# A context attention that keeps 32 keys: wider weights and masks, three small operations moved, the last group turned in two parts

## The chip, the cores and the metric

The kernel runs on one core of one Trainium2 chip, as one launch. Its time is the device time of that core in microseconds (us). TensorE multiplies matrices into PSUM, VectorE does elementwise work and reductions, ScalarE functions and copies, GpSimd (POOL in the profile) elementwise work on SBUF; SyncE (SP) issues most DMAs. In the profile PEld is TensorE's loading of the stationary operand, DVE is VectorE and ACT is ScalarE.

## What is computed

The reference is a small network of two layers on 4 batches of 256 tokens, with 4096 context tokens of 192 numbers a batch. The change lies in one step, the context attention of the second layer. Cut to that step:

```python
Q = (x_text @ Wq).reshape(Bb, Tt, H, DH)            # H = 4 heads of 32
K = (x_vision @ Wk).reshape(Bb, Gg, H, DH)          # 4096 keys from 192 numbers each
scores = jnp.einsum('bthd,bghd->bhtg', Q, K) / np.sqrt(DH)
scores = jnp.where(vision_mask[:, None, None, :], scores, -jnp.inf)
topv, topi = jax.lax.top_k(scores, 32)
probs = jax.nn.softmax(topv, axis=-1)
attn = jnp.zeros_like(scores).at[bi, hi, ti, topi].set(probs)
attn_mean = attn.mean(axis=1)                       # over the heads
V = x_vision @ Wv
c_t = jnp.einsum('btg,bgd->btd', attn_mean, V) * text_mask[..., None]
```

Each token and head keeps the 32 best of 4096 keys, and the softmax runs over these alone. `c_t` then steers the rest of the layer. Everything is in float32 except the mask.

## The kernel before

The step is `l1_context`, with `l1_context_keys` for the keys. It runs over 32 **units**: 4 batches, 2 tiles of 128 tokens, 4 heads. The four heads of one tile form a **group**; there are 8 groups. A unit goes through these steps:

- `scores(u)` (TensorE, two halves `c2` of 2048 keys): the 4096 scores of 128 tokens. Each half fills two PSUM tiles of 128x1024; ScalarE copies each to SBUF (`sc`, L1164). The pool `x1_sc` has eight such tiles, so two units' worth. The PSUM pool `big` has two tiles, so a half can begin only as the tiles of the half before are copied.
- `best(u, part)` (VectorE): the 8 largest of every 128 scores, 16 operations of 128 elements for each half (L1176).
- `chosen(u)`: from these 256 candidates VectorE takes the 32 best, 8 at a time (L1184, L1189). After the first 8 it writes `neg`, minus the largest score (L1187). ScalarE then takes the exponential of all scores with `neg` as bias, in four operations of 1024 (L1191), and of the 32 best (`e32`, L1193).
- `weighted(u)` (VectorE): the mask, in four operations of 1024 (L1200): a weight stays where its score is at least the 32nd best. Then the sum of `e32` (L1202), its reciprocal (L1203), and the factor 0.25 for the mean over the heads times the token's `keep` flag (L1204). POOL writes `diag`, the identity scaled by that number for each token (L1206).
- `gathered` (once a group, in four steps `c4` of 1024 keys): TensorE turns the weights of all four heads with `diag` as the moving operand (L1219), which transposes, scales and sums over the heads at once. ScalarE copies the result (`wT`, L1227) and TensorE multiplies it with the context (`cx`, L1233) into one PSUM tile `ps_c`. It yields after each turning and after each product, so a group is eight pieces. At its end come a copy `o`, a check `off` on VectorE (L1241) and a DMA of `o` to `c.cn`.

The weights of one group fill all sixteen tiles `e`. `weights(u)` hands the tiles out row by row in one group and column by column in the next, so that a unit of the next group may write its exponentials as soon as one step `c4` of the running `gathered` has read its tiles.

The order of the work is written out by hand in the loop over `u`: `chosen(u)`, first half of `best(u + 1)`, `weighted(u)`, second half of `best(u + 1)`, one piece of the running `gathered` (`late`), first half of `scores(u + 2)`, one piece of `late`, second half of `scores(u + 2)`, then one or two pieces of `keys(b + 1)` for the next batch. At the fourth head of a group what is left of `late` is run out and the group just weighted becomes the new `late`. After the last unit nothing is left beside the last group's `gathered` but loads for the next stage, which begins with a branch on `c.bad` and reads `c.cn`. The framework beneath places the semaphores by the parts of tiles that operations touch, and may move operations of one engine past each other when it plans the order.

`keys(b)` makes the keys of one batch in eight chunks of 512: the 192 context numbers are contracted as 128 rows (L1049) and as 64 rows (L1050), the latter from the upper or the lower half of the array by turns. The context comes by `context_keys` in tiles of 128 x 1536 numbers, four a batch, two buffered (L247); `load_kk` loads the weights for this layout with three DMAs. ScalarE copies each chunk (`ks`, L1052) and SP writes it to the `kt` tile in four DMAs (L1054). The first batch's keys are made before `l0_ffn`, the others beside the units.

Of the kernel before, what the change touches and what calls it, by code (L numbers as in the profile page):

```python
# [11 lines left out]
F32 = mybir.dt.float32  # L12
# [9 lines left out]
P = 128  # L22
# [209 lines left out]
def mask_rows(c, pool, mu):  # L232
# [10 lines left out]
def context_keys(c, pool, b, c4, queue=None):  # L243


    t = pool.tile([P, 1536], F32, tag="ctxT", name="ctxT")
    (queue or c.nc.sync).dma_start(t, c.a["ctxT"][b, c4])  # L247
    return t


def load_kk(c, pool, name, queue=None):
# [770 lines left out]
def l1_context_keys(c, es):  # L1022

    nc, tc = c.nc, c.tc
    w = Ctx()
    one = es.enter_context(tc.tile_pool(name="x1_kt", bufs=1))
    two = es.enter_context(tc.tile_pool(name="x1_ks", bufs=2))
    w.psum = es.enter_context(tc.tile_pool(name="x1_ps", bufs=1, space=PSUM))
    w.wk = load_kk(c, one, "x1_wku")
    w.wq = load_k(c, one, "x1_wq4")  # L1030
    w.keep = load(c, one, "x1_keep", [P, NB], dt=U8)
    w.kts = [one.tile([P, 4, G // 4], F32, tag=f"kt{i}", name=f"kt{i}") for i in range(2)]

    w.mask = one.tile([P, G // 4], BF16, tag="mask", name="mask")
    nc.vector.memset(w.mask, 0.0)
    w.pick = one.tile([P, B, P], BF16, tag="pick", name="pick")
    for b in range(B):
        nc.sync.dma_start(w.mask[b:P:32, :], c.mrowb[b].rearrange("(j k) -> j k", j=4))
        nc.vector.tensor_copy(w.pick[:, b, :], c.cols[:, 5 + b : 6 + b].to_broadcast([P, P]))

    def keys(b):

        kt = w.kts[b % 2]
        for c4 in range(4):
            ctxT = context_keys(c, two, b, c4)
# [12 lines left out]

    w.keys = keys
    return w  # L1060


def l1_context(c, w, beside):
# [13 lines left out]
    with ExitStack() as es:  # L1077
# [11 lines left out]
        nc.vector.tensor_copy(keep, w.keep)  # L1089
        off = one.tile([P, NB], F32, tag="off", name="off")  # L1090
# [51 lines left out]
        def scores(u):  # L1142

            b, tt, h = units[u]
            kt = w.kts[b % 2]
            sc[u] = []
            for c2 in range(2):
                cs = slice(c2 * 512, (c2 + 1) * 512)
                pss = [big.tile([P, 2, 512], F32, tag="big", name="ps_s") for _ in range(2)]
                for j in range(4):  # L1150
                    rs = slice(32 * j, 32 * j + 32)
                    nc.tensor.matmul(pss[j // 2][:, j % 2, :], w.pick[rs, b, :], w.mask[rs, cs], start=True, stop=False)
                for j in range(4):
                    rs = slice(32 * j, 32 * j + 32)
                    nc.tensor.matmul(  # L1155
                        pss[j // 2][:, j % 2, :],
                        qs[b][rs, h, tt * P : (tt + 1) * P],
                        kt[rs, h, cs],
                        start=False,
                        stop=True,  # L1160
                    )
                for ps in pss:
                    t = scs.tile([P, 2, 512], F32, tag="sc", name="sc")
                    nc.scalar.copy(t, ps)  # L1164
                    sc[u].append(t)
                yield

        sc, cands = {}, {}
# [1 line left out]
        def best(u, part):  # L1170

            if part == 0:
                cands[u] = two.tile([P, 32, 8], F32, tag="cand", name="cand")
            for n in range(16 * part, 16 * part + 16):
                c4, i = divmod(n, 8)
                nc.vector.max(cands[u][:, n, :], sc[u][c4][:, i // 4, (i % 4) * P : (i % 4 + 1) * P])  # L1176

        def chosen(u):

            top = two.tile([P, 32], F32, tag="top", name="top")  # L1180
            flat = cands.pop(u).rearrange("p n k -> p (n k)")
            for r in range(4):
                t8 = top[:, 8 * r : 8 * r + 8]
                nc.vector.max(t8, flat)  # L1184
                if r == 0:
                    neg = two.tile([P, 1], F32, tag="neg", name="neg")
                    nc.vector.tensor_scalar(neg, top[:, 0:1], -1.0, None, ALU.mult)  # L1187
                if r < 3:
                    nc.vector.match_replace(flat, t8, flat, TAKEN)  # L1189
            for t, src in zip(weights(u), sc[u]):  # L1190
                nc.scalar.activation(t, src, AF.Exp, bias=neg)  # L1191
            e32 = two.tile([P, 32], F32, tag="e32", name="e32")
            nc.scalar.activation(e32, top, AF.Exp, bias=neg)  # L1193
            return top, e32

        def weighted(u, top, e32):

            b, tt, h = units[u]
            for t, src in zip(weights(u), sc.pop(u)):
                nc.vector.scalar_tensor_tensor(t, src, top[:, 31:32], t, ALU.is_ge, ALU.mult)  # L1200
# [5 lines left out]
            nc.gpsimd.tensor_scalar(diag, c.ident, r, None, ALU.mult)  # L1206
            return weights(u), diag

        def gathered(b, tt, es):

            ps_c = acc.tile([P, 512], F32, tag="acc", name="ps_c")
            n = 0
            for c4 in range(4):
                wTs = []
                for half in range(2):
                    ps = pst.tile([P, 512], F32, tag="pt", name="ps_w")
                    for i in range(4):
                        for h, (e, diag) in enumerate(es):
                            nc.tensor.matmul(  # L1219
                                ps[:, i * P : (i + 1) * P],  # L1220
                                e[c4][:, half, i * P : (i + 1) * P],
                                diag,
                                start=(h == 0),
                                stop=(h == 3),
                            )
                    wT = two.tile([P, 512], F32, tag="wT", name="wT")
                    nc.scalar.copy(wT, ps)  # L1227
# [2 lines left out]
                for half, wT in enumerate(wTs):  # L1230
                    for i in range(4):
                        t, j = c4 % 2 * 2 + half, c4 // 2 * 4 + i
                        nc.tensor.matmul(  # L1233
                            ps_c[:, : DC + 1], wT[:, i * P : (i + 1) * P], cxs[b][t][:, j, :], start=(n == 0), stop=(n == 31)
                        )
# [17 lines left out]
        for u, (b, tt, h) in enumerate(units):  # L1253
# [774 lines left out]
def _arrays(i):  # L2028
# [11 lines left out]
    for m in range(P):  # L2040
# [13 lines left out]
    ctxT = i["ctx_768"].transpose(0, 2, 1).reshape(B, DC, 4, 2, 512)  # L2054
    ctxT = np.concatenate(
        [ctxT[:, 0:P].transpose(0, 2, 1, 3, 4).reshape(B, 4, P, 1024), ctxT[:, P:].transpose(0, 2, 3, 1, 4).reshape(B, 4, P, 512)], 3
    )
    return {
        "x": i["x"],
        "ctx": i["ctx_768"],  # L2060
        "ctxT": ctxT,
        "ctx6": i["ctx_768"].reshape(B, 4, 4, 256, 6, 32).transpose(0, 1, 2, 5, 4, 3).reshape(B, 4, P, 6, 256),
        "gmask": i["mask_BxS2_bf1"].view(np.uint8),
        "cols": cols,
# [78 lines left out]
```

## Time and profile before

| what | value |
|---|---|
| median of 3 runs | 2594.22 us (2590.08 to 2595.49) |
| profiled execution | 2598.63 us, of which span 2596.8 us |
| busy over the span | PE 2377.7 us (92%), PEld 1460.1 (56%), DVE 1659.8 (64%), ACT 1064.9 (41%), POOL 145.2 (6%) |
| mean granted TensorE clock | 0.935 |
| first and last mask (L1200) | 1626.3 and 2145.6 us from the start |
| last product with cx (L1233) | ends at 2182.8 us |
| first and last keys chunk | 1507.5 and 1999.9 us |

The page has a strip of the busy tenths of each engine in 40 slices of 65 us. The units lie in slices 26 to 33; the last of these holds the end of the last group:

```
PE   6999999999999999999688989989999988984897
DVE  6666666666666666678544423988888892725644
PEclk7999999999999999999799799999799998996876
```

A matmul of float32 stands as two records in the trace, so L1219 counts 2048 for 1024 matmuls. A row of a group gives the line, engine and operation, what it writes and reads with sizes, the count, then busy time and the mean of one in ns, and last the idle time of the engine ahead of it and what ended that. A row of the order of time gives start, length, the operation, and in brackets the idle time before it. A clock of 0.5 means that TensorE ran at half its speed.

### The profile page before, as it was taken

The page shows a single profiled execution, that of the slowest core. Times are in us where ns is not written, and L with a number is a line of the kernel's source. Part 1 is how long each engine was busy: PE and PEld are TensorE (multiplying, and loading weights), DVE is VectorE, ACT ScalarE, POOL GpSimd, SP SyncE. Part 2 cuts the span into 40 slices and gives each one's busy share as a digit, 9 for nine tenths or more (in the row PEclk, how much of TensorE's full clock was granted, in tenths as well). Part 3 has the DMA queues.
Part 4 walks back from the last instruction along what each step waited for, and adds up shares of the span by engine and source line. Part 5 has one row for each costly group of instructions (what it writes and reads, how often), then busy time and mean ns, then how long its engine had stood idle before and what let it go on. Part 6 is the DMA issues. An engine that isn't in the chain of part 4 may idle for free. (4 is left out here: it accounts for less than half of the span.)

```text
span 2596.8 us, 54625 instructions
## 1 busy us (share of the span) xinstructions
PE 2377.7 (92%) x22673; PEld 1460.1 (56%) x22673; DVE 1659.8 (64%) x4019; ACT 1064.9 (41%) x1865; POOL 145.2 (6%) x176
## 2 busy tenths in 40 slices
PE   6999999999999999999688989989999988984897
PEld 4655555555555555545455535467676777453554
DVE  6666666666666666678544423988888892725644
ACT  1355554555555554556122121755555651010221
POOL 3000000000000000000000000001011010412000
PEclk7999999999999999999799999799999998996876
DMA  8321213121221213000100031202212004000110
GB/s 208 91 57 58 66 49 79 43 75 48 67 56 59 75 40 81 28 8 2 38 5 1 1 116 57 61 27 73 64 51 59 27 27 143 14 1 16 33 25 9
DMA packets 63375, 132.29 MB, mean 51 GB/s; under 512 B 11744, under 2 KB 38560, under 8 KB 62672
## 3 DMA queue, kind: packets, MB, share of 16 engines
q1 hardware_dynamic: 61616, 124.65, 17.1%
q8 instruction: 181, 2.97, 0.5%
q10 hardware_dynamic: 992, 3.02, 0.4%
q0 software_dynamic: 512, 1.05, 0.2%
q14 instruction: 74, 0.61, 0.1%
HBM read 98.17 MB, written 5.34 MB: 40 GB/s over the span
## 5 line engine op out<-in xcount | busy, mean ns | idle before, releaser
L512 DVE TENSOR_REDUCE mx<-ps_a 128x1 f32<-128x512 f32 x1024 | 659.7, 685 | 223.6 <-PE ps_a L497 220.0
L508 ACT ACTIVATE e<-ps_s 128x512 f32<-128x512 f32 x1024 | 555.7, 595 | 418.1 <-PE ps_a L497 397.8
L497 PE MATMUL ps_a<-kt,qa 32*128 32x512 f32 x2048 | 659.5, 647 | 12.0 <-DVE mx L512 8.1
L483 PE MATMUL ps_s<-qb,kt 32*128 32x256 f32 x4096 | 592.4, 401 | 0.0
L483 PEld LDWEIGHTS ps_s<-qb,kt 32*128 32x128 f32 x4096 | 349.6, 184 | 197.5 <-issue 106.6
L425 PE MATMUL o_ps<-e,v 128*32 128x256 f32 x4096 | 327.6, 391 | 0.0
L497 PEld LDWEIGHTS ps_a<-kt,qa 32*128 32x128 f32 x2048 | 230.9, 185 | 41.8 <-DVE mx L512 19.7
L1219 PEld LDWEIGHTS ps_w<-diag,e 128*128 128x128 f32 x2048 | 240.0, 198 | 24.6 <-issue 22.4
L1219 PE MATMUL ps_w<-diag,e 128*128 128x128 f32 x2048 | 245.8, 282 | 1.4 <-POOL diag L1206 1.4
L1176 DVE MAX8 cand<-sc 128x8 f32<-128x128 f32 x1024 | 212.3, 277 | 11.7 <-ACT sc L1164 10.2
L425 PEld LDWEIGHTS o_ps<-e,v 128*32 128x32 f32 x4096 | 81.0, 108 | 246.5 <-issue 235.0
L1200 DVE SCALAR_TENSOR_TENSOR e<-sc,top,e 128x1024 f32<-128x1024 f32 x128 | 159.3, 1279 | 31.9 <-ACT e L1191 31.9
L1191 ACT ACTIVATE e<-sc,neg 128x1024 f32<-128x1024 f32 x128 | 143.1, 1146 | 33.0 <-PE ps_w L1219 32.4
L1164 ACT COPY sc<-ps_s 128x1024 f32<-128x1024 f32 x128 | 126.1, 1006 | 46.2 <-PE ps_s L1155 45.6
L329 PE MATMUL ps_k<-ctxT,x_wk 32*128 32x256 f32 x1536 | 103.3, 398 | 12.3 <-DMA ctxT<-in_ctx 12.3
L351 PEld LDWEIGHTS ps_v<-x_wv,ctxT 32*128 32x128 f32 x3072 | 97.9, 191 | 15.4 <-DVE mx L512 9.4
L351 PE MATMUL ps_v<-x_wv,ctxT 32*128 32x128 f32 x3072 | 105.1, 280 | 0.7
L1233 PEld LDWEIGHTS ps_c<-cx,wT 128*128 128x128 f32 x512 | 88.0, 199 | 27.6 <-ACT wT L1227 11.4
L329 PEld LDWEIGHTS ps_k<-ctxT,x_wk 32*128 32x128 f32 x1536 | 87.7, 194 | 26.8 <-issue 18.2
L1233 PE MATMUL ps_c<-cx,wT 128*128 128x193 f32 x512 | 99.7, 347 | 2.0 <-ACT wT L1227 2.0
L814 POOL TENSOR_TENSOR x<-x,f_bo 128x256 f32<-128x256 f32 x8 | 5.8, 724 | 1547.6 <-DVE x L813 1520.4
L1155 PE MATMUL ps_s<-kt,q 32*128 32x512 f32 x512 | 85.8, 657 | 0.0
(401 smaller groups left out, 2520.0 us busy)
## 6 DMA issues: line engine op xcount, KB each, us to landing
ctxT<-in_ctx SPq DMA_DIRECT2D x62, 768.0 KB
kt<-ks SPq DMA_DIRECT2D x352, 64.0 KB
ctxT<-in_ctxT SPq DMA_DIRECT2D x16, 768.0 KB
cx<-in_ctx SPq DMA_DIRECT2D x16, 768.0 KB
x_w<-in_x_w SPq DMA_DIRECT2D x2, 1024.0 KB
qk<-rot SPq DMA_DIRECT2D x8, 256.0 KB
a_qk<-qk SPq DMA_DIRECT2D x16, 128.0 KB
ctxT<-in_ctx ACTq DMA_DIRECT2D x2, 768.0 KB
```

Source lines behind the costliest of these rows:

```text
L329: nc.tensor.matmul(ps[:, :256], w.wk[hs, gp, k, :], ctxT[hs, k, :], start=(k == 0), stop=(k == 5))
L351: nc.tensor.matmul(ps[:, ks], ctxT[hs, k, ks], w.wv[hs, gp, k, :], start=(k == 0), stop=(k == 5))
L425: nc.tensor.matmul(o_pss[u][32 * h : 32 * h + 32, :S], vs[g // 2][:, c0 : c0 + 32], ew[h][:, n % 2, :], start=(n == 0), stop=(n == GT - 1),)
L483: nc.tensor.matmul(ps[:, k * S : (k + 1) * S], kts[u % 4 // 2][hs, u % 2, ks], qbs[u][hs, :], start=True, stop=True,)
L497: nc.tensor.matmul(ps, qas[u][hs, tt * P : (tt + 1) * P], kts[u % 4 // 2][hs, u % 2, ch * 512 : (ch + 1) * 512], start=True, stop=True,)
L508: nc.scalar.activation(e, ps.rearrange("p (k n) -> p k n", k=2), AF.Exp)
L512: nc.vector.tensor_reduce(mxs[u][:, tt, h, ch : ch + 1], ps, AX.X, ALU.max)
L1176: nc.vector.max(cands[u][:, n, :], sc[u][c4][:, i // 4, (i % 4) * P : (i % 4 + 1) * P])
L1191: nc.scalar.activation(t, src, AF.Exp, bias=neg)
L1200: nc.vector.scalar_tensor_tensor(t, src, top[:, 31:32], t, ALU.is_ge, ALU.mult)
L1219: nc.tensor.matmul(ps[:, i * P : (i + 1) * P], e[c4][:, half, i * P : (i + 1) * P], diag, start=(h == 0), stop=(h == 3),)
L1233: nc.tensor.matmul(ps_c[:, : DC + 1], wT[:, i * P : (i + 1) * P], cxs[b][t][:, j, :], start=(n == 0), stop=(n == 31))
```

## The change

It has five parts, all in the context attention of the second layer.

1. The sixteen tiles `e` become one tile of 16 x 1024, and `sc` becomes four tiles of 2048. Exponentials and masks are done 2048 at a time: two of each a unit in place of four. The score copies stay at 1024 each, two into one tile. `weights(u)` hands out the same places as before.
2. The negation `neg` goes from VectorE to POOL.
3. The sum of `e32` is taken by ScalarE's accumulating output as it computes the exponential; the factor 0.25 and `keep` are multiplied once for all tiles (`quarter`) and enter `diag` on POOL as a second multiplication. VectorE's reduction and its scaling of `r` go.
4. The keys are contracted as twice 96 rows. The context is laid out for that (`ctx96`), loaded in chunks of 96 x 1024 numbers, eight a batch, still two buffered; the weights come in one DMA.
5. The last group (units 28 to 31) is turned in two parts. At units 29 and 30 two more pieces of `late` are run each, at unit 30 the group before is run out, and the first two heads are turned and multiplied with `cx` while the last heads are still being chosen. The last two heads follow, and add to the same PSUM tile.

```diff
-    w.wk = load_kk(c, one, "x1_wku")
+    w.wk = one.tile([96, 2, P], F32, tag="x1_wku", name="x1_wku")
+    nc.sync.dma_start(w.wk, c.a["x1_wku"].rearrange("(k p) n -> p k n", p=96))
...
-            ctxT = context_keys(c, two, b, c4)
             for j in range(2):
-                hs = slice(64 * j, 64 * j + 64)
+                ctx = two.tile([96, 2, 512], F32, tag="ctx", name="ctx")
+                nc.sync.dma_start(ctx, c.a["ctx96"][b, 2 * c4 + j])
                 ps = w.psum.tile([P, 512], F32, tag="mm", name="ps_k")
-                nc.tensor.matmul(ps, w.wk[:, 0, :], ctxT[:, j * 512 : (j + 1) * 512], start=True, stop=False)
-                nc.tensor.matmul(ps, w.wk[hs, 1, :], ctxT[hs, 1024:1536], start=False, stop=True)
+                for k in range(2):
+                    nc.tensor.matmul(ps, w.wk[:, k, :], ctx[:, k, :], start=(k == 0), stop=(k == 1))
...
-        scs = last.enter_context(tc.tile_pool(name="x1_sc", bufs=8))
+        scs = last.enter_context(tc.tile_pool(name="x1_sc", bufs=4))
...
+        nc.vector.tensor_scalar(quarter, keep, 0.25, None, ALU.mult)
...
-        tiles = [ews.tile([P, 2, 512], F32, tag=f"e{i}", name=f"e{i}") for i in range(16)]
+        tiles = ews.tile([P, 16, 1024], F32, tag="e", name="e")
...
-            return [tiles[4 * c4 + h if odd else 4 * h + c4] for c4 in range(4)]
+            return tiles[:, h:16:4, :] if odd else tiles[:, 4 * h : 4 * h + 4, :]
...
-                for ps in pss:
-                    t = scs.tile([P, 2, 512], F32, tag="sc", name="sc")
-                    nc.scalar.copy(t, ps)
-                    sc[u].append(t)
+                t = scs.tile([P, 2, 1024], F32, tag="sc", name="sc")
+                for j, ps in enumerate(pss):
+                    nc.scalar.copy(t[:, j, :], ps.rearrange("p q n -> p (q n)"))
+                sc[u].append(t)
...
-                    nc.vector.tensor_scalar(neg, top[:, 0:1], -1.0, None, ALU.mult)
+                    nc.gpsimd.tensor_scalar(neg, top[:, 0:1], -1.0, None, ALU.mult)
...
-            for t, src in zip(weights(u), sc[u]):
-                nc.scalar.activation(t, src, AF.Exp, bias=neg)
+            for part, src in enumerate(sc[u]):
+                nc.scalar.activation(weights(u)[:, 2 * part : 2 * part + 2, :], src, AF.Exp, bias=neg)
...
-            nc.scalar.activation(e32, top, AF.Exp, bias=neg)
+            nc.scalar.activation(e32, top, AF.Exp, bias=neg, accum_out=r)
...
-            for t, src in zip(weights(u), sc.pop(u)):
+            for part, src in enumerate(sc.pop(u)):
+                t = weights(u)[:, 2 * part : 2 * part + 2, :]
                 nc.vector.scalar_tensor_tensor(t, src, top[:, 31:32], t, ALU.is_ge, ALU.mult)
-            r = two.tile([P, 1], F32, tag="r", name="r")
-            nc.vector.tensor_reduce(r, e32, AX.X, ALU.add)
             nc.vector.reciprocal(r, r)
-            nc.vector.tensor_scalar(r, r, 0.25, keep[:, 2 * b + tt : 2 * b + tt + 1], ALU.mult, ALU.mult)
...
-            nc.gpsimd.tensor_scalar(diag, c.ident, r, None, ALU.mult)
+            nc.gpsimd.tensor_scalar(diag, c.ident, r, quarter[:, i : i + 1], ALU.mult, ALU.mult)
...
-        def gathered(b, tt, es):
+        def gathered(b, tt, es, ps_c, first, last):
...
-                                stop=(h == 3),
+                                stop=(h == len(es) - 1),
...
+                            start=(first and n == 0),
+                            stop=(last and n == 31),
...
+            if not last:
+                return
...
             next(late, None)
+            if u == n - 3 or u == n - 2:
+                for _ in range(2):
+                    next(late, None)
+            if u == n - 2:
+                for _ in late:
+                    pass
+                ps_c = acc.tile([P, 512], F32, tag="acc", name="ps_c")
+                late = gathered(b, tt, group[:2], ps_c, True, False)
+                for _ in range(4):
+                    next(late, None)
             if h == 3:
...
-                late = gathered(b, tt, group)
+                if u == n - 1:
+                    late = gathered(b, tt, group[2:], ps_c, False, True)
+                else:
+                    late = gathered(b, tt, group, acc.tile([P, 512], F32, tag="acc", name="ps_c"), True, True)
```

More of the change, by code (lines that the diff above doesn't have):

```diff
@@ L240, in mask_rows @@
     nc.sync.dma_start(c.mrowb.rearrange("b (a k) -> (b a) k", k=S), mb)
[L243 to L248, printed above, removed]
 def load_kk(c, pool, name, queue=None):
@@ L1085, in l1_context @@
         last = es.enter_context(ExitStack())
-        scs = last.enter_context(tc.tile_pool(name="x1_sc", bufs=8))
+        scs = last.enter_context(tc.tile_pool(name="x1_sc", bufs=4))
         keep = one.tile([P, NB], F32, tag="keep", name="keep")
         nc.vector.tensor_copy(keep, w.keep)
+        quarter = one.tile([P, NB], F32, tag="quarter", name="quarter")
+        nc.vector.tensor_scalar(quarter, keep, 0.25, None, ALU.mult)
         off = one.tile([P, NB], F32, tag="off", name="off")
-        tiles = [ews.tile([P, 2, 512], F32, tag=f"e{i}", name=f"e{i}") for i in range(16)]
+        tiles = ews.tile([P, 16, 1024], F32, tag="e", name="e")
         def weights(u):
             h, odd = u % 4, u // 4 % 2
-            return [tiles[4 * c4 + h if odd else 4 * h + c4] for c4 in range(4)]
+            return tiles[:, h:16:4, :] if odd else tiles[:, 4 * h : 4 * h + 4, :]
         def tokens(b):
@@ L1173, in best @@
                 cands[u] = two.tile([P, 32, 8], F32, tag="cand", name="cand")
-            for n in range(16 * part, 16 * part + 16):
-                c4, i = divmod(n, 8)
-                nc.vector.max(cands[u][:, n, :], sc[u][c4][:, i // 4, (i % 4) * P : (i % 4 + 1) * P])
+            for n in range(16):
+                j, i = divmod(n, 8)
+                nc.vector.max(cands[u][:, 16 * part + n, :], sc[u][part][:, j, i * P : (i + 1) * P])
         def chosen(u):
@@ L1186, in chosen, with weighted @@
                     neg = two.tile([P, 1], F32, tag="neg", name="neg")
-                    nc.vector.tensor_scalar(neg, top[:, 0:1], -1.0, None, ALU.mult)
+                    nc.gpsimd.tensor_scalar(neg, top[:, 0:1], -1.0, None, ALU.mult)
                 if r < 3:
                     nc.vector.match_replace(flat, t8, flat, TAKEN)
-            for t, src in zip(weights(u), sc[u]):
-                nc.scalar.activation(t, src, AF.Exp, bias=neg)
+            for part, src in enumerate(sc[u]):
+                nc.scalar.activation(weights(u)[:, 2 * part : 2 * part + 2, :], src, AF.Exp, bias=neg)
             e32 = two.tile([P, 32], F32, tag="e32", name="e32")
-            nc.scalar.activation(e32, top, AF.Exp, bias=neg)
-            return top, e32
-        def weighted(u, top, e32):
+            r = two.tile([P, 1], F32, tag="r", name="r")
+            nc.scalar.activation(e32, top, AF.Exp, bias=neg, accum_out=r)
+            return top, r
+        def weighted(u, top, r):
             b, tt, h = units[u]
-            for t, src in zip(weights(u), sc.pop(u)):
+            for part, src in enumerate(sc.pop(u)):
+                t = weights(u)[:, 2 * part : 2 * part + 2, :]
                 nc.vector.scalar_tensor_tensor(t, src, top[:, 31:32], t, ALU.is_ge, ALU.mult)
-            r = two.tile([P, 1], F32, tag="r", name="r")
-            nc.vector.tensor_reduce(r, e32, AX.X, ALU.add)
             nc.vector.reciprocal(r, r)
-            nc.vector.tensor_scalar(r, r, 0.25, keep[:, 2 * b + tt : 2 * b + tt + 1], ALU.mult, ALU.mult)
             diag = two.tile([P, P], F32, tag=f"diag{h}", name=f"diag{h}")
-            nc.gpsimd.tensor_scalar(diag, c.ident, r, None, ALU.mult)
+            i = 2 * b + tt
+            nc.gpsimd.tensor_scalar(diag, c.ident, r, quarter[:, i : i + 1], ALU.mult, ALU.mult)
             return weights(u), diag
-        def gathered(b, tt, es):
-            ps_c = acc.tile([P, 512], F32, tag="acc", name="ps_c")
+        def gathered(b, tt, es, ps_c, first, last):
             n = 0
@@ L1220, in gathered @@
                                 ps[:, i * P : (i + 1) * P],
-                                e[c4][:, half, i * P : (i + 1) * P],
+                                e[:, c4, half * 512 + i * P : half * 512 + (i + 1) * P],
                                 diag,
                                 start=(h == 0),
-                                stop=(h == 3),
+                                stop=(h == len(es) - 1),
                             )
@@ L1233, in gathered @@
                         nc.tensor.matmul(
-                            ps_c[:, : DC + 1], wT[:, i * P : (i + 1) * P], cxs[b][t][:, j, :], start=(n == 0), stop=(n == 31)
+                            ps_c[:, : DC + 1],
+                            wT[:, i * P : (i + 1) * P],
+                            cxs[b][t][:, j, :],
+                            start=(first and n == 0),
+                            stop=(last and n == 31),
                         )
@@ L2053, in _arrays @@
     causal[:, 1] = causal[:, 0].T
[L2054 to L2057, printed above, removed]
     return {
@@ L2060, in _arrays @@
         "ctx": i["ctx_768"],
-        "ctxT": ctxT,
+        "ctx96": i["ctx_768"].transpose(0, 2, 1).reshape(B, 2, 96, 8, 512).transpose(0, 3, 2, 1, 4),
         "ctx6": i["ctx_768"].reshape(B, 4, 4, 256, 6, 32).transpose(0, 1, 2, 5, 4, 3).reshape(B, 4, P, 6, 256),
```

## Prediction

> **What bounds the stage.** I read the granted clock of the core first (0.935 over the span), then the page's groups of instructions, then busy time by stretch, then the order of time inside one unit. A unit is one head of one 128-token tile of one batch; there are 32.
>
> ```profile
> L1219 PE MATMUL ps_w<-diag,e 128*128 128x128 f32 x2048 | 245.8, 282 | 1.4 <-POOL diag L1206 1.4
> L1176 DVE MAX8 cand<-sc 128x8 f32<-128x128 f32 x1024 | 212.3, 277 | 11.7 <-ACT sc L1164 10.2
> ...
> L1200 DVE SCALAR_TENSOR_TENSOR e<-sc,top,e 128x1024 f32<-128x1024 f32 x128 | 159.3, 1279 | 31.9 <-ACT e L1191 31.9
> L1191 ACT ACTIVATE e<-sc,neg 128x1024 f32<-128x1024 f32 x128 | 143.1, 1146 | 33.0 <-PE ps_w L1219 32.4
> L1164 ACT COPY sc<-ps_s 128x1024 f32<-128x1024 f32 x128 | 126.1, 1006 | 46.2 <-PE ps_s L1155 45.6
> ```
>
> The page looks like a VectorE stage: VectorE picks (L1176) and masks (L1200). But the last columns say that the mask waits for the exponential and the exponential for TensorE's turning matmuls (L1219). The stretches (PE, weight load, DVE, ACT, POOL busy, clock, DMA) tell where which engine is full:
>
> ```profile
> 1622.00:1723.00 101.00, 89.34 (x444) 49.25 (x443) 100.28 (x363) 68.95 (x81) 6.30 (x7) 0.81 0.19 55
> 1723.00:2030.00 307.00, 282.19 (x1905) 213.85 (x1906) 256.56 (x866) 169.22 (x210) 27.10 (x25) 0.94 0.19 53
> 2030.00:2104.00 74.00, 66.12 (x505) 55.41 (x503) 70.63 (x242) 44.67 (x54) 9.38 (x9) 0.95 0.16 45
> 2104.00:2147.00 43.00, 39.47 (x312) 36.02 (x308) 39.97 (x130) 24.30 (x30) 3.81 (x3) 0.96 0.01 4
> 2147.00:2183.00 36.00, 35.79 (x291) 35.49 (x289) 1.47 (x4) 4.86 (x9) 0.00 (x0) 1.00 0.28 94
> ```
>
> VectorE is full only in the first 101 us. From 1723 on TensorE has 92% (282.19 of 307) and VectorE loses 50 us; the last 36 us are TensorE alone, turning the last group. One unit without key projection, in order of time:
>
> ```profile
> 2096.32 1.15 ACT L1191 ACTIVATE e<-sc,neg 128x1024 f32<-128x1024 f32 x1 [0.66 <-PE ps_w L1219]
> 2097.37 0.57 ACT L1227 COPY wT<-ps_w 128x512 f32<-128x512 f32 x1
> 2097.84 2.19 ACT L1191 ACTIVATE e<-sc,neg 128x1024 f32<-128x1024 f32 x2
> ...
> 2099.93 0.99 ACT L1164 COPY sc<-ps_s 128x1024 f32<-128x1024 f32 x1
> 2100.82 1.15 ACT L1191 ACTIVATE e<-sc,neg 128x1024 f32<-128x1024 f32 x1
> 2101.87 1.00 ACT L1164 COPY sc<-ps_s 128x1024 f32<-128x1024 f32 x1
> ...
> 2102.92 0.39 PE L1152 MATMUL ps_s<-mask,pick 32*128 32x512 bf16 x2 [1.56 <-ACT sc L1164]
> 2102.93 1.24 PE L1155 MATMUL ps_s<-kt,q 32*128 32x512 f32 x8
> 2104.10 1.14 PE L1219 MATMUL ps_w<-diag,e 128*128 128x128 f32 x4
> ```
>
> This is a ring without VectorE in it: turning ends (2096.9), ScalarE works without a gap for 6.55 us (four exponentials, one wT copy, two score copies), TensorE gets its score bank back, does 1.2 us of scores and turns again for 7.4. Sum from exponential to exponential 14.6 to 14.8 us; VectorE's unit takes as long by chance.
>
> **The change, part by part** (against the profiled execution: span 2596.8, 1.8 around it, 2598.6 in all, 4.4 above the median of the runs).
>
> *Masks 2048 wide and small operations off VectorE.* Three masks back to back take 3.70, so 1.23 each and 4.93 a unit. The same operation takes 289 ns at 128 elements (L824) and 1279 at 1024: 1.105 ns an element, so 2.41 at 2048, 4.73 for two with the same overlap: 0.20 saved. With only the 0.15 us beyond the elements going it would be 0.30; I take 0.25. The reduction goes (0.20 start to start), the scaling of r (0.13 until the mask starts), the negation (only 0.07: the next load lies over it). 0.65 a unit, 21 us in all. It is worth that only where VectorE sets the pace: units 0 to 6, some **-4.5**, of which I keep **-4** as TensorE idles under 1 us in three of them. From 1723 on it goes into VectorE's waiting.
>
> *The negation on POOL.* No row shows a [128,1] operation there; a POOL fill of 128x8 takes 0.11, the 128x128 scaling 0.60. The Trainium skill, "GPSIMD Engine Reference", section 3, speaks against the move: POOL is roughly half as fast for elementwise work. By that the 0.154 becomes an estimated 0.31, 5 us over 32 units if exposed. The row decides: the negation at 2091.73 has its first reader at 2096.32, since that waits for turning. 0 lost, up to +5. Queued behind it are only the scaled identities and the fills of cx; one fill waited 12.7 us for TensorE, and a negation caught behind such a fill would hold all exponentials. The fills came 3 us or more before the next negation; I take 0.
>
> *Exponentials 2048 wide.* 320 ns at 32 elements (L1193) and 1146 at 1024 give 0.833 ns an element and 2.00 us at 2048; the four in the ring cost 4.20, two would cost 3.82, so -0.38. But the first now rewrites two heads' weights and must wait for one more turning matmul (7.41 us for 32, 0.23): net -0.15 on the ring, bounds -0.4 and +0.2. Some 24 units: **-3.5**. The first mask can start only after 2.0 us in place of 1.15; that makes VectorE wait 0.8 in units where it waits already, beside TensorE. The e32 sum moves into ScalarE: no row has the extra output; 32 x 0 to 0.2 us in ScalarE's idle time. Score buffers: two units' worth as before, but one is released by a mask twice as wide; the next copy into it came 3.5 us after the second mask's end (1895.7, 1899.3), so 0.
>
> *Keys.* Before, a 128-row and a 64-row matmul alternate: 1909.43, 1910.49, 1911.54, that is 1.05 each. Two of the same 128 rows follow each other in 1.92 for both (L803 at 1529.58, next line at 1531.50), 0.96 each. With 96 rows twice there is no change of rows inside a chunk or behind it: -0.2 for each of 24 chunks, of which the TensorE-bound ones keep **-3** (bounds 0, -5). SP issues eight half-size loads a batch in place of four, and one load of the weights for three; each load may start only two half-chunks ahead. Chunks are a unit (some 15 us) apart and the loads' share of the DMA engines is 0.2: 0, up to +3 where they stand behind the 3 MB of cx on SP.
>
> *Last group in two parts.* It is turned in 4 steps of 9.75 us:
>
> ```profile
> 2172.86 7.31 PE L1219 MATMUL ps_w<-diag,e 128*128 128x128 f32 x64
> 2180.00 2.79 PE L1233 MATMUL ps_c<-cx,wT 128*128 128x193 f32 x16
> ```
>
> Turning is shared between the parts, but the product with cx (2.45 to 2.8 a step) must be done for each: 4 x 2.55 = **+10.2 us of TensorE work**. The tail after the last mask would shrink from 36 to about 25, if the first part fitted in before. It doesn't: from 2104 to the end TensorE idles only 3.9 us (2.0 before scores, 1.95 before a wT copy). Filling those: +10.2 - 3.9 = **+6** (bounds +3, +12: the first product of part one waits for `off` on VectorE, which came up to 4.7 us behind the last product, and scores of the last unit move behind two turning steps).
>
> *The clock.* After the pause of 1.56 us above:
>
> ```profile
> 2104.00:2108.00 4.00, 4.00 (x24) 3.90 (x21) 3.86 (x18) 1.93 (x2) 0.00 (x0) 0.57 0.02 4
> ```
>
> that turning took 9.04 in place of 7.41. The Trainium skill, "TensorE: Matmul & The Clock Gate", part 1, asks for a whole idle window of about 3.4 us before the clock halves; by that rule these pauses cost only themselves. By the row each may cost 1.7 more: between 1723 and 2147 the mean clocks (0.94, 0.95, 0.96) make some 48 us at half clock, in eleven stretches, 24 us lost. The measurement decides. A ring shorter by 0.15 and filled pauses at the end may spare one or two: **-2** (bounds -24, +6, as it is the moment of the pause that counts).
>
> Sum: -4 - 3.5 - 3 + 6 - 2 = -6.5; 2598.6 - 6.5 = 2592 for the profiled execution, 2594.2 - 6.5 = **2588 for the median**.
>
> **Rivals.** *The pauses go.* If on ScalarE the score copies come ahead of the second wide exponential, TensorE resumes 2 us sooner in some ten units, and half of the 24 us at half clock go: -6.5 - 10 - 10, about 2568. For it: score copies already stand between exponentials. Against: at the moment of choice (exponential and wT done, 2.6 us after the turn) the old order took an exponential. *Slower: the split on a full TensorE.* The place is 2104 to the end: +10.2 with little filled, +2 for the wait on `off`, and the ring gains nothing since the wide exponential starts later: 2604. It decides once TensorE's idle time from unit 28 on is under the 10 us that the split adds; the stretches above speak for it, the gains elsewhere against. *The change cancels out*: parts work and end within 2 us of 2594.
>
> **Chances.** Own case 0.42 (2580 to 2595), pauses go 0.20 (2560 to 2580), slower 0.26 (2600 to 2615), cancelled 0.12. Under 0.2% (5.2 us) a difference can't be told from none. Faster: 0.20 + about 0.22 of the own case; slower 0.26 + 0.03. So 0.42, 0.29, 0.29. The range 2567 to 2606 leaves out a tenth at each end.
>
> **What would show it.** Masks of 2.35 to 2.41 us, exponentials of 2.0; VectorE busy some 20 us less, but idle time before L1200 not less. Pitch of units without keys 14.4 to 14.7. 512 products with cx become 576. The tail with VectorE idle 25 to 27 us in place of 36, and it starts later than the 2147 of before, less what the stage gained. Wrong if the pitch falls to 14.0 (VectorE was in the ring), if the half-clock stretches vanish, or if TensorE idles over 3 us between 2104 and its end.

## The result, and the profile after

| | before | changed |
|---|---|---|
| median of the runs, us | 2594.35 | 2609.24 |
| ratio to before, 95% interval | | 1.0047, 1.0026 to 1.0067 |
| the same, in a second set of runs | | 1.0018, 1.0008 to 1.0028 |
| span of the profiled execution, us | 2596.8 | 2609.3 |
| granted clock over the span | 0.935 | 0.934 |
| VectorE / TensorE busy, us | 1659.8 / 2377.7 | 1639.0 / 2380.3 |

The change makes the kernel slower, by 0.2 to 0.5%. The forecast was 2588 and a range up to 2606. In the second set (medians 2605.2 and 2598.3) the interval lies above 1 too, but reaches below the 0.2% under which the prediction called a difference too small to tell. Ratios are taken over all runs but those far slower than the rest (in this set one of 3468 us of the changed kernel and one of 8743 us of the kernel before), and not from the medians.

The groups of instructions of the changed kernel that answer to those shown of before (columns as there: busy time, mean ns of one, idle time of the engine before them and what ended it):

```profile
L1213 PE MATMUL ps_w<-diag,e 128*128 128x128 f32 x2048 | 240.6, 278 | 0.0
L1171 DVE MAX8 cand<-sc 128x8 f32<-128x128 f32 x1024 | 209.7, 276 | 18.5 <-ACT sc L1159 18.5
L1197 DVE SCALAR_TENSOR_TENSOR e<-sc,top,e 128x2048 f32<-128x2048 f32 x64 | 150.1, 2354 | 40.2 <-ACT e L1186 39.7
L1159 ACT COPY sc<-ps_s 128x1024 f32<-128x1024 f32 x128 | 123.6, 1013 | 42.2 <-PE ps_s L1150 37.9
L1186 ACT ACTIVATE e<-sc,neg 128x2048 f32<-128x2048 f32 x64 | 128.2, 2005 | 25.2 <-PE ps_w L1213 19.7
L1227 PE MATMUL ps_c<-cx,wT 128*128 128x193 f32 x576 | 107.7, 338 | 5.1 <-ACT wT L1221 5.0
```

The operations cost what the prediction made of them: masks 2354 ns, exponentials 2005, VectorE 20.8 us less busy, 576 records of products in place of 512. VectorE's idle time ahead of the masks went up, from 31.9 to 40.2. None of these lines says that the kernel is slower.

The stretches do. They are cut here at the negations that start a unit: units 0 to 6, 7 to 23, 24 to 28, 29 and 30, and the last unit up to the last `off` (columns: PE, weight load, DVE, ACT, POOL busy, clock, DMA share, GB/s):

```profile
1628.76:1727.51 98.75, 87.86 (x444) 52.79 (x443) 96.55 (x328) 65.96 (x74) 4.86 (x15) 0.81 0.20 57
1727.51:2032.40 304.89, 276.05 (x1916) 213.94 (x1917) 245.73 (x781) 163.72 (x193) 12.07 (x43) 0.94 0.20 56
2032.40:2104.53 72.13, 64.94 (x523) 54.13 (x522) 69.33 (x227) 44.80 (x51) 3.74 (x14) 1.00 0.16 46
2104.53:2142.55 38.02, 34.95 (x275) 31.44 (x274) 28.29 (x92) 17.61 (x21) 1.31 (x4) 0.96 0.01 3
2142.55:2192.54 49.99, 47.62 (x362) 46.94 (x360) 9.02 (x16) 13.69 (x21) 0.66 (x2) 1.00 0.20 68
```

Set against the same stretches of before, in the two profiled executions:

| stretch | before | changed | difference |
|---|---|---|---|
| start to first negation | 1622.4 | 1628.8 | +6.4 |
| units 0 to 27 | 469.4 | 461.4 | -8.0 |
| units 28 to 30 | 45.5 | 52.4 | +6.9 |
| last negation to last `off` | 46.1 | 50.0 | +3.9 |
| behind it | 413.5 | 416.8 | +3.3 |
| sum | 2596.8 | 2609.3 | +12.5 |

Two of these hold code that the change does not touch. The stage before the second layer ends at 1496.2 in the one execution and at 1499.8 in the other; over all kernels run here it ends between 1496.2 and 1501.0. The part behind the last `off` takes 411.9 to 417.3. So 3.6 of the first row and the 3.3 of the last are of the size by which executions differ. What belongs to the change is +2.8 before the units, -8.0 in them, and +10.8 at the end.

The end is the place of part 5. In the loop's step for unit 29 two extra pieces of the group before stand on TensorE ahead of the scores of unit 31. They come to run as VectorE begins unit 30. The changed kernel in order of time (here and below, rows of other operations are left out):

```profile
2119.80 1.48 PE L1227 MATMUL ps_c<-cx,wT 128*128 128x193 f32 x8
2121.21 0.39 PE L1147 MATMUL ps_s<-mask,pick 32*128 32x512 bf16 x4
2122.16 1.99 ACT L1186 ACTIVATE e<-sc,neg 128x2048 f32<-128x2048 f32 x1
2124.05 0.56 ACT L1221 COPY wT<-ps_w 128x512 f32<-128x512 f32 x1
2124.67 2.94 PE L1227 MATMUL ps_c<-cx,wT 128*128 128x193 f32 x8 [3.07 <-ACT wT L1221]
2127.54 1.16 PE L1150 MATMUL ps_s<-kt,q 32*128 32x512 f32 x8
2129.79 3.19 DVE L1171 MAX8 cand<-sc 128x8 f32<-128x128 f32 x16 [0.88 <-ACT sc L1159]
```

The second half of a product waits for its `wT` copy, which stands on ScalarE behind an exponential of 1.99. TensorE pauses 3.07 us, and the next product runs at half clock (2.94 for 8 records, 1.48 just before). The scores at 2127.54 wait behind it, and VectorE, which needs them, idles 9.1 us in unit 30. That gave two theories: **products** (the split's 32 extra products are paid in full on a full TensorE) and **order** (the late scores are the loss).

### The profile page after: what moved, and what is told of

Its sections match the earlier page's. It is cut to its first block, busy times and chain, and to the rows that moved or that the text cites. A ratio compares the mean times of both kernels' runs of the same rounds, so it can differ in the third digit from the quotient of the medians.

```text
span 2609.3 us, 54644 instructions
## 1 busy us (share of the span) xinstructions
PE 2380.3 (91%) x22737; PEld 1474.6 (57%) x22737; DVE 1639.0 (63%) x3860; ACT 1059.4 (41%) x1841; POOL 121.3 (5%) x208
## 5 line engine op out<-in xcount | busy, mean ns | idle before, releaser
L1197 DVE SCALAR_TENSOR_TENSOR e<-sc,top,e 128x2048 f32<-128x2048 f32 x64 | 150.1, 2354 | 40.2 <-ACT e L1186 39.7
L1186 ACT ACTIVATE e<-sc,neg 128x2048 f32<-128x2048 f32 x64 | 128.2, 2005 | 25.2 <-PE ps_w L1213 19.7
L1227 PEld LDWEIGHTS ps_c<-cx,wT 128*128 128x128 f32 x576 | 98.8, 196 | 26.0 <-issue 17.5
L1227 PE MATMUL ps_c<-cx,wT 128*128 128x193 f32 x576 | 107.7, 338 | 5.1 <-ACT wT L1221 5.0
L1043 PE MATMUL ps_k<-ctx,x_wku 96*128 96x512 f32 x128 | 77.9, 738 | 13.0 <-ACT ks L1045 12.4
```

What stands on the lines that cost most here:

```text
L1186: nc.scalar.activation(weights(u)[:, 2 * part : 2 * part + 2, :], src, AF.Exp, bias=neg)
L1227: nc.tensor.matmul(ps_c[:, : DC + 1], wT[:, i * P : (i + 1) * P], cxs[b][t][:, j, :], start=(first and n == 0), stop=(last and n == 31),)
```

## The experiments

Each ratio is to runs of the kernel before on the same chip; of the times, only these ratios are compared between chips. The traces divide every kernel at the same three points: (a) from the end of the stage before, the last point that no kernel changes, to the first negation; (b) units 0 to 27; (c) unit 28 to the last `off`.

| kernel | (a) us | (b) us | (c) us | ratio, 95% interval |
|---|---|---|---|---|
| before | 126.2 | 469.4 | 91.6 | |
| changed | 128.9 | 461.4 | 102.4 | 1.0047, 1.0026 to 1.0067 |
| changed_again | 128.9 | 461.4 | 102.4 | 1.0018, 1.0008 to 1.0028 |
| wide_only | 125.9 | 467.0 | 92.8 | 0.9994, 0.9983 to 1.0006 |
| one_part | 128.9 | 461.3 | 89.9 | 0.9985, 0.9975 to 0.9996 |
| old_keys | 126.3 | 463.8 | 102.7 | 1.0042, 1.0028 to 1.0055 |
| keys_only | 129.4 | 464.9 | 90.9 | 0.9988, 0.9980 to 0.9996 |
| scores_first | 128.8 | 460.9 | 101.8 | 1.0017, 1.0005 to 1.0029 |
| scores_first_again | 129.0 | 461.3 | 100.3 | 1.0018, 1.0006 to 1.0031 |
| no_products | 130.1 | 458.6 | 90.4 | 0.9983, 0.9974 to 0.9993 |
| keys_3buf | 124.1 | 460.3 | 91.2 | 0.9971, 0.9956 to 0.9987 |
| neg_vector | 124.6 | 460.2 | 89.9 | 0.9970, 0.9959 to 0.9980 |
| narrow | 128.4 | 466.9 | 94.7 | 0.9998, 0.9983 to 1.0013 |
| exp_narrow | 128.2 | 474.8 | 94.3 | 1.0045, 1.0030 to 1.0060 |

**Which part it is.** Four kernels take the change apart; they ran on one chip. one_part takes part 5 out of the changed kernel:

```diff
-            if u == n - 3 or u == n - 2:
...
-            if u == n - 2:
...
-                if u == n - 1:
-                    late = gathered(b, tt, group[2:], ps_c, False, True)
-                else:
-                    late = gathered(b, tt, group, acc.tile([P, 512], F32, tag="acc", name="ps_c"), True, True)
+                late = gathered(b, tt, group, acc.tile([P, 512], F32, tag="acc", name="ps_c"), True, True)
```

> The changed kernel with the last group turned in one part, as before. Theory 'split': the split costs what unit 30 and the tail grew by, 8.8 + 3.9 = 12.7 us: 2596.5 (2594 to 2599). Theory 'keys': the split is nearly free and the loss stands before the units: 2605 or more. Theory 'wide': 2605 or more too.

old_keys takes part 4 out, wide_only takes 4 and 5 out, and keys_only is the kernel before with part 4. The lines of part 4, as keys_only adds them:

```diff
-            ctxT = context_keys(c, two, b, c4)
...
+                ctx = two.tile([96, 2, 512], F32, tag="ctx", name="ctx")
+                nc.sync.dma_start(ctx, c.a["ctx96"][b, 2 * c4 + j])
```

> The changed kernel with keys as before (128 and 64 rows, loads of 768 KB). Theory 'split': still slow; the 6.4 us before the first unit come back in part (3), the chunks in the units lose 3: 2606 to 2610. Theory 'keys': the 6.4 us come back whole and nothing is lost: 2600 to 2603.

> The kernel before with parts 1 to 3 alone (weights and masks 2048 wide, negation and scaling off VectorE); keys and last group as before. Theory 'split': these parts are sound and earn what units 0 to 27 earned in the changed kernel, 8.0 us, less some 3 that its keys had in it: 2589 (2585 to 2592). Theory 'wide': the longer exponential holds the first mask back and the loss is in these parts: 2600 or more. Theory 'keys': the gain in units 0 to 27 was the keys' alone: 2593 to 2595.

> The kernel before with the keys alone contracted as twice 96 rows. Theory 'split': +3 before the units, -3 in them: 2593 to 2597. Theory 'keys': the start costs 6.4 and the units give back little: 2598 to 2601.

Both kernels with the split are slow and both without it are not. With the old keys the split costs 1.0042 - 0.9994 = 0.0048 of 2597, 12.5 us, and the intervals lie apart. In column (c) it is 102.4 against 89.9 with the new keys. Keys alone are worth 3 us (0.9988); that refutes the theory that they are the loss. one_part came out lower than its theory had it (0.9985 of 2594.35 is 2590.5, expected 2594 to 2599). wide_only missed its 2589: parts 1 to 3 alone show no gain that can be measured. Their trace has -2.4 in (b); 1.2 of it is lost again in (c), where 6.8 us of the last unit fell to half clock.

**Why the split costs.** TensorE's groups in stretch (c), and the stretch's busy times, of the changed kernel:

```profile
L1213 PE MATMUL ps_w<-diag,e 128*128 128x128 f32 x487 | 56.7, 275 | 0.0
L1227 PE MATMUL ps_c<-cx,wT 128*128 128x193 f32 x192 | 35.8, 338 | 4.9 <-ACT wT L1221 4.8
L1147 PE MATMUL ps_s<-mask,pick 32*128 32x512 bf16 x20 | 2.4, 383 | 1.4 <-ACT sc L1159 1.4
```

```profile
2090.11:2192.54 102.43, 95.55 (x739) 89.20 (x737) 51.15 (x152) 40.22 (x52) 2.63 (x8) 0.98 0.11 36
```

and of the kernel in one part:

```profile
L1213 PE MATMUL ps_w<-diag,e 128*128 128x128 f32 x487 | 56.0, 275 | 0.0
L1227 PE MATMUL ps_c<-cx,wT 128*128 128x193 f32 x128 | 22.9, 329 | 3.1 <-ACT wT L1221 3.1
L1147 PE MATMUL ps_s<-mask,pick 32*128 32x512 bf16 x20 | 2.7, 382 | 2.9 <-ACT sc L1159 2.9
```

```profile
2087.23:2177.11 89.88, 83.38 (x675) 77.68 (x673) 50.71 (x152) 35.30 (x44) 2.66 (x8) 1.00 0.12 41
```

Turning is the same work (487 records). The products went from 128 records to 192, from 22.9 to 35.8 us. TensorE's idle time, stretch less busy, is 6.5 us with one part and 6.9 with two, so the split used up none of it on balance. The pauses moved: the extra pieces filled one of the two pairs of pauses ahead of scores (L1147: 2.9 us became 1.4), but brought a wait for a `wT` copy of their own (L1227: 3.1 became 4.9). Two kernels put this to the test. scores_first moves the extra pieces of unit 29 behind the scores:

```diff
-            if u == n - 3 or u == n - 2:
+            if u == n - 2:
...
             next(ahead, None)
+            if u == n - 3:
+                for _ in range(2):
+                    next(late, None)
```

> The changed kernel; at unit 29 the two extra pieces come behind the scores of unit 31, not ahead of them. Theory 'products': TensorE is full, the split's 32 extra products are paid whichever way they stand; VectorE gets unit 31 some 8 us sooner, and the end does not move by more than 3: 2606 to 2610. Theory 'order': the 8.8 us of unit 30 were the scores' place behind turning, and come back: 2599 to 2602.

Here is the answer of its second run for the same two stretches as the last two lines of the changed kernel above (units 29 and 30, the last unit):

```profile
2105.65:2134.85 29.20, 27.76 (x231) 24.71 (x230) 27.69 (x91) 16.49 (x19) 1.31 (x5) 1.00 0.00 1
2134.85:2191.52 56.67, 53.27 (x406) 52.71 (x405) 9.18 (x17) 14.57 (x23) 0.65 (x2) 1.00 0.18 62
```

Units 29 and 30 take 29.2 in place of 38.0, so VectorE did get its scores 9 us sooner. The last unit then takes 56.7 in place of 50.0: the pieces taken out ahead of it are done in it, on a TensorE that is busy 53.3 of the 56.7. The two together gain 2.1: 1.6 us of products at half clock and some idle time. The ratio 1.0017 lay between the two theories, so the kernel was run again beside the changed one:

> The changed kernel itself, on the same chip as the next three. Every theory: what was measured, 1.0047 of the time before, within its interval: 1.003 to 1.006.

> The changed kernel with unit 31's scores ahead of the extra pieces, beside the changed kernel on the same chip. Theory 'products': the last off of the first look came only 1.1 us sooner (2191.4 against 2192.5, with the same first negation); the difference is 0 to 3 us. Theory 'order': the look before gave 1.0017, some 8 us less than the changed kernel, and a good half of the split's cost is the order: 6 to 9 us less.

Both came to 1.0018, for the changed kernel below the 1.003 to 1.006 expected: the order is worth nothing that the times can tell, and 2.1 us in the trace. no_products keeps the split and its order, and leaves out the products of the first part (the last 128 tokens lack two heads, and the two others count double; the lines that double them are not shown):

```diff
-                for half, wT in enumerate(wTs):
+                for half, wT in enumerate(wTs if last else []):
```

> The changed kernel without the products of the last group's first part: its two heads are turned but not multiplied, and the last two heads count double. Left out: those heads' share of the last 128 tokens. Theory 'products': 64 records with 193 columns less, 11.5 us and one half-clock stretch: 2596 to 2599. Theory 'order': the wait in unit 30 stays, only the tail is shorter by 3 to 4: 2604 to 2607.

It is as fast as one part: 0.9983, and 90.4 against 89.9 in (c). It still has the wait in unit 30, where its VectorE idles 7.5 us. That settles it: the extra products are the loss, 64 records and 12 us, and the late scores cost little beside them.

**Why the keys cost 3 us before the units.** In column (a) every kernel with the new keys in two buffers is near 129, those with the old near 126. The kernel before, around the router of the layer before:

```profile
1520.51 1.12 PE L1050 MATMUL ps_k<-ctxT,x_wku 64*128 64x512 f32 x2
1522.89 1.03 PE L793 MATMUL ps_kt<-ident,kept 128*32 128x128 f32 x8 [1.26 <-DVE kept L783]
```

The changed kernel in the same place:

```profile
1513.56 8.49 SPq L1047 DMA_DIRECT2D kt<-ks  x12
...
1517.00 1.95 PE L1043 MATMUL ps_k<-ctx,x_wku 96*128 96x512 f32 x4 [0.40 <-DMA ctx<-in_ctx]
...
1522.15 1.02 SPq L1040 DMA_DIRECT2D ctx<-in_ctx  x2
1525.47 1.86 PE L785 MATMUL ps_kt<-ident,kept 128*32 128x128 f32 x8 [3.24 <-DVE kept L775]
```

```profile
1523.50:1530.30 6.80, 4.83 (x12) 2.22 (x12) 1.65 (x14) 1.15 (x2) 0.00 (x0) 0.50 0.40 111
```

Before, the chunks of keys filled the time in which TensorE waits for the router on VectorE. Now a load brings one chunk, not two, so that two buffers are two chunks ahead and not four. The fourth load stands on SP behind twelve copies of keys and is issued at 1522.15. When the router comes, TensorE has three chunks behind it, where it had four, and no fourth to do. It pauses 3.24 us in place of 1.26, and the clock falls to 0.50 for 6.8 us. The pause itself makes nothing later: `kept` is turned 25.6 us after the end of the stage before, against 26.7 in the kernel before. The loss comes behind it, a chunk still to do and some 3.4 us by the half clock. keys_3buf (one part, and one more buffer) tests it:

```diff
-                ctx = two.tile([96, 2, 512], F32, tag="ctx", name="ctx")
+                ctx = two.tile([96, 2, 512], F32, tag="ctx", name="ctx", bufs=3)
```

> The changed kernel with the last group in one part, and three buffers for the context loads in place of two. Theory 'loads': the keys of batch 0 cost 2.9 us before the units, as the third half-chunk's load waits on SP behind copies of keys and TensorE is left without work for 3.2 us and goes to half clock; with one more load ahead that goes: 2591 to 2593, no half-clock stretch at 1520 to 1527. Theory 'noise': no stretch depends on it: 2594 to 2596.

```profile
1519.65 1.96 PE L1043 MATMUL ps_k<-ctx,x_wku 96*128 96x512 f32 x4
...
1523.06 1.03 PE L785 MATMUL ps_kt<-ident,kept 128*32 128x128 f32 x8 [1.45 <-DVE kept L775]
```

```profile
1520.00:1530.00 10.00, 8.55 (x25) 3.27 (x24) 2.71 (x28) 2.72 (x6) 0.00 (x0) 1.00 0.29 73
```

A fourth chunk stands ahead of the router again, the pause is 1.45 and the clock stays at 1.00; (a) falls from 128.9 to 124.1. At 0.9971 this kernel is faster than the one before and than the changed one. Against one_part (0.9985, another chip) the intervals overlap, so its 4.8 us rest on the trace.

**What the wide form is worth.** narrow is one_part with exponentials and masks 1024 wide; exp_narrow has only the exponentials narrow.

```diff
-                nc.scalar.activation(weights(u)[:, 2 * part : 2 * part + 2, :], src, AF.Exp, bias=neg)
+                for j in range(2):
+                    nc.scalar.activation(weights(u)[:, 2 * part + j, :], src[:, j, :], AF.Exp, bias=neg)
```

> The changed kernel with the last group in one part, and exponentials and masks 1024 wide again; negation, sum and scaling stay off VectorE. My prediction's steps: the wide exponentials and masks earned 3.5 and part of 4: 2598 to 2600. Theory 'first mask late': the wide exponential gives its first mask 0.85 us later, which costs where VectorE had caught up (units 5 to 7, units with keys), as much as the shorter ring earns: 2593 to 2596.

> The changed kernel with the last group in one part and exponentials 1024 wide, masks still 2048. Theory 'ring' (my step): the exponentials alone earn the shorter ring, so the pitch of units without keys goes from 14.43 back to 14.57 and the pauses of TensorE from 0.91 and 0.53 back to one of 1.57: 2597 to 2600, nearly as the kernel with both narrow. Theory 'masks': the gain of the wide form is VectorE's: 2594 to 2596, with a pitch of 14.43.

The time of narrow (0.9998) can't be told from that of one_part (0.9985, another chip), so it settles neither of its theories. Its trace has 96.3 us at half clock between first negation and last `off`, one_part's 72.2: some 12 us lost, more than what was to be measured. The pitch, from one negation to the next, is clear of that in the units without keys that had the full clock: 14.75 before, 14.57 narrow, 14.43 with both wide, and 15.03 with wide masks behind narrow exponentials (16.0 to 16.2 where a half-clock stretch fell). That last one I had at 14.57 or 14.43; neither theory held, and at 1.0045 it is the one kernel in one part that is slower than the one before. Its unit:

```profile
2045.00 1.15 ACT L1187 ACTIVATE e<-sc,neg 128x1024 f32<-128x1024 f32 x1
...
2046.05 0.57 ACT L1222 COPY wT<-ps_w 128x512 f32<-128x512 f32 x1
...
2046.52 2.19 ACT L1187 ACTIVATE e<-sc,neg 128x1024 f32<-128x1024 f32 x2
...
2047.71 2.35 DVE L1198 SCALAR_TENSOR_TENSOR e<-sc,top,e 128x2048 f32<-128x2048 f32 x1 [1.20 <-ACT e L1187]
2048.61 1.00 ACT L1159 COPY sc<-ps_s 128x1024 f32<-128x1024 f32 x1
...
2049.50 1.16 ACT L1187 ACTIVATE e<-sc,neg 128x1024 f32<-128x1024 f32 x1
...
2050.76 2.33 DVE L1198 SCALAR_TENSOR_TENSOR e<-sc,top,e 128x2048 f32<-128x2048 f32 x1
...
2051.61 0.39 PE L1147 MATMUL ps_s<-mask,pick 32*128 32x512 bf16 x2 [1.56 <-ACT sc L1159]
```

A wide mask must wait for two exponentials, and ScalarE puts a `wT` copy (2046.05) or a score copy (2048.61) between them; VectorE waits 1.20 us for the first. In the changed kernel the same unit runs:

```profile
2050.69 2.00 ACT L1186 ACTIVATE e<-sc,neg 128x2048 f32<-128x2048 f32 x1
2052.60 0.57 ACT L1221 COPY wT<-ps_w 128x512 f32<-128x512 f32 x1
2052.73 4.73 DVE L1197 SCALAR_TENSOR_TENSOR e<-sc,top,e 128x2048 f32<-128x2048 f32 x2 [0.36 <-ACT e L1186]
2053.07 2.01 ACT L1186 ACTIVATE e<-sc,neg 128x2048 f32<-128x2048 f32 x1
2054.97 1.91 ACT L1159 COPY sc<-ps_s 128x1024 f32<-128x1024 f32 x2
2056.03 0.39 PE L1147 MATMUL ps_s<-mask,pick 32*128 32x512 bf16 x2 [0.92 <-ACT sc L1159]
2056.94 0.39 PE L1147 MATMUL ps_s<-mask,pick 32*128 32x512 bf16 x2 [0.52 <-ACT sc L1159]
```

Both score copies now stand together behind the exponentials, and TensorE's pause of 1.56 has become two of 0.92 and 0.52. So in these units the wide masks alone cost 0.46 a unit (14.57 to 15.03) and the wide exponentials bring 0.60; together they gain 0.14. In units 12, 14, 20 and 22, which lie between keys, narrow has 14.76 and both wide 15.14: there the wide form costs 0.38. Wide exponentials with narrow masks were not run.

**The negation.** neg_vector is keys_3buf with `nc.vector` in place of `nc.gpsimd` for `neg`.

> The kernel with one part and three buffers, with the negation back on VectorE. My prediction's step was 0 for the move to POOL (0 to +5): VectorE's pitch where it sets the pace grows by 0.07 in units 0 to 3, elsewhere nothing moves: within 1 us of 0.9971 of the time before. If POOL's start held the exponentials up, it is faster by 1 to 5.

0.9970 beside 0.9971; the pitch is 13.30 in place of 13.26 where VectorE sets it, and 14.47 in place of 14.43 in the ring. The move to POOL costs nothing. The negation itself took 0.21 us on POOL where VectorE took 0.15, 1.4 times as long; the factor of two that the prediction took from the Trainium skill, "GPSIMD Engine Reference", section 3, stands there for an addition of two inputs of 2048 numbers.

## Why the prediction was wrong

- **Last group in two parts, +6: the step that failed** is the idle time that was to cover the added work. The prediction put "4 x 2.55 = +10.2 us of TensorE work" less 3.9 of idle time: "+10.2 - 3.9 = +6". The added products came to 11.3 us where no half clock fell on them (34.2 against 22.9 in scores_first_again), a little over the 10.2. But the idle time was not used up: from unit 28 on it is 6.5 us in the kernel with one part and 6.9 with two. A pause on TensorE here is an instruction at the head of its queue that waits for ScalarE (a score bank, a `wT` copy). The pieces that stood ahead of the scores did fill 1.4 us of such pauses; then the first product of part one waited 1.70 us for its own `wT` copy. Behind the scores they filled nothing (scores_first_again idles 6.3). The sum should have been +11 to +13; it was +12.5 in the trace, 1.6 of it products at half clock.
- **The signs of that step.** TensorE idles 5.4 us from 2104 on, over the 3 that were to show the step wrong; but the kernel with one part has 5.1 there and the kernel before had 3.9, so this sign could not tell them apart. The wait on `off`, which I had allowed 2 us, cost nothing: `off` was written at 2142.4, the first product of part one came at 2145.3, behind its `wT`. And the tail after the last mask is not 25 to 27 us but 42.5 (2150.05 to 2192.54). The prediction had itself said that the first part would not fit in before; by the end of the last mask only the first of its four steps was done.
- **The slower rival** named this mechanism and this place and gave 2604. Its rule was that the split decides once TensorE's idle time from unit 28 on is under the 10 us it adds, and the prediction's own 2.0 + 1.95 from 2104 on answered it. I read that as cover to be used up; even filled whole it left +6. Two other terms of this rival did not come, the wait on `off` and a ring that gains nothing. **The pauses go** did not come either: both score copies stand behind the second wide exponential.
- **VectorE, -4.** Its pitch in units 2 and 3 fell by 0.53 (13.79 to 13.26), of which the small operations are 0.27 (narrow 13.52) where I had 0.40, and the width 0.26 where I had 0.25. The stage of units 0 to 6 gained 2.0, half of what I put down: units 5 and 6 together became longer (30.25 to 31.43), as VectorE idles 2.17 us in them where it idled 0.34. The later first mask, which I had named as a cost, is 0.74 of that; narrow idles 1.63 there without it.
- **Exponentials, -3.5.** The ring lost 0.14 between narrow and wide, as predicted (0.15), for the pair and not for the exponentials. Another 0.18 (14.75 to 14.57 between negations) is not the ring's. In keys_only, with exponentials and masks as before, the turning starts every 14.57 already, while VectorE, busy 72.55 of 73.72 us in units 24 to 28, is what the negations follow (4.59 us ahead of their exponential in unit 24, 3.88 in unit 28):

```profile
2034.35:2108.07 73.72, 65.83 (x530) 55.02 (x530) 72.55 (x251) 46.57 (x56) 13.17 (x9) 1.00 0.16 45
```

That VectorE's unit took as long as the ring "by chance" was therefore a wrong reading: in these units it was the slower of the two, and its small operations counted there too. Between keys the unit became longer (14.88 to 15.14).
- **Keys, -3, loads 0 to +3.** In the units -2.4 to -5.6 (column (b), old_keys and wide_only against the kernels with the new keys), and +2.6 to +3.2 for the loads (column (a)), at the end of the range I had not taken, and in a place where I had not looked: before the units, where nothing but chunks of keys covered a pause.
- **The negation, 0.** Right.
- **The clock, -2.** Half-clock time between the first negation and the last `off` went from 85.9 to 75.6 us, some 5 us less lost, all of it in units 0 to 27. In units 24 to 28 it went from 9.1 to 0, but so it did in keys_only, where the ring is as before. It is not shown to be the work of any part, and that it helped was luck.

The forecast had +6 for the split and -12.5 for the rest. In the profiled executions the stretches that the change touches came to 2.8 - 8.0 + 10.8 = +5.6, near what the second set of runs shows (6.8 between the medians, 2 to 7 by the interval). The 12.1 between -6.5 and +5.6 are +6.5 for the split, +2.8 for the loads ahead of the units, and +4.5 for units 0 to 27, which gained 8.0 where 12.5 was forecast, some 5 of the 8.0 by the clock; less 1.7 that the other parts gained from unit 28 on (91.6 before, 89.9 in one part). The rest of the 12.5 between the profiled executions lies in code that the change leaves alone, as far as these two executions show.

## What to carry to other kernels

Before a reduction is split so that its first part can run early, add up the work that is then done twice on the engine that carries the tail. Idle time of that engine is no cover by itself: if it consists of waits for another engine, ask which of them an extra piece would stand ahead of, and what waits the piece brings with it. Here the two cancelled and the extra work added in full. When a load is cut in half, its buffers reach half as far ahead: count the work that the loads in flight cover, not the buffers. Do not widen a consumer without its producer: here a wide mask waited for both narrow exponentials and for the copy that stood between them.

## What was not expected of the hardware

Whether a pause halves the clock is not told by its length. Before, units 24 to 28 had pauses of 1.56 us and 76.26 us in all at a mean clock of 0.94, with 1.2 to 2.3 us at half clock in each unit. The kernel with the keys alone has the same instructions and the same pause in those units, and takes 73.72 at 1.00. The Trainium skill, "TensorE: Matmul & The Clock Gate", part 1, says that the window the gate looks at runs free, and that the moment of its change therefore depends on where the work falls in it; this pair agrees with that, though the idle window it asks for (about 3.4 us) is twice the pause after which the clock fell here. Longer pauses tell no more: the wait of 3.07 to 3.09 us for a `wT` copy near the end was followed by 3.4 us at half clock in the changed kernel, by none in one_part and by 6.8 in wide_only. What the traces do have in common is the length: the half-clock stretches between first negation and last `off` are all multiples of 3.41 us. Over the kernels of the table the half-clock time between first negation and last `off` lies between 58 and 96 us, some 19 us of lost time between the ends, and a part worth 3 us can't be read from one time of each of two kernels beside that. The changed kernel showed the same stretches in two executions (75.6 and 75.7 us); scores_first showed two patterns (13.8 and 10.2 us at half clock in unit 0).
